# Two groups of small products on TensorE, each made one section of the schedule

## The chip, the cores and the metric

The kernel runs on one core of one Trainium2 chip. Its engines are TensorE (PE in the profile, with its weight loads as PEld), VectorE (DVE), ScalarE (ACT), GpSimd (POOL) and SyncE (SP); the last one here only issues DMAs. The metric is device time in microseconds of one execution, and the median of three runs stands for a kernel.

## What is computed

One block of a network on four sequences of 512 tokens and 256 channels: a state-space mixer with adaptive layer norm, then a gated feed-forward layer. What the change touches is the mixer's inner product. Cut to that, the reference is:

```python
Lm = jnp.exp(segsum(a))                                # decay from token s to token l, 0 for s > l
M = jnp.einsum('blhn,bshn,bhls->bhls', Cm, Bm, Lm)     # C against B over 64 states, times the decay
y = jnp.einsum('bhls,bshp->blhp', M, x)                # applied to x, 8 channels a head
```

There are 32 heads. B and C come from a projection of the normalized input, then a causal convolution over four tokens.

## The kernel before

The sum over s is cut into chunks of Q = 64 tokens. Within a chunk the product is computed as written (C times B, times the decay, times x); across chunks a state is carried. So a sequence has NC = 8 chunks.

**Tiling.** Two heads make a pair, numbered k from 0 to NP = 64: eight pairs for a unit n, which is one half of the heads of one sequence; there are eight units. Four pairs make a quad m, numbered 0 to 15. For each pair:

- `project(k, 0)` and `project(k, 1)` compute B and C: six 512-column matmuls each by `proj` (L266) into a PSUM tile (`pbc`, `pcc`), and `conv` (L400 to L407) turns each into an SBUF tile `bc` or `cc`, with two instructions on ScalarE, two on VectorE and one on GpSimd.
- `prep_l(k)` (L440) makes the decay tile `l` with one matmul and an exponential.
- `attend(k)` (L457) is called for odd k alone and takes the pairs k-1 and k. For each of 8 chunks, 2 pairs and 2 heads it issues one 64x64x64 product of C and B at one of the four 64x64 positions of the array, into the PSUM tiles `pG` of the two pairs: 32 matmuls. VectorE then multiplies each `pG` into its `l` (L473).
- `turn_b(k)` (L475) transposes `bc`, for the states.

For each quad, `intra(m)` (L552) applies the four `l` tiles to x: for each of 8 chunks and 4 pairs one matmul of 128 rows, 32 columns and 64 elements, 32 in all, into the PSUM tile `py` (L561). `states(m)` (`ps`, L545) and `inter(m)` (`pi`, L587) carry the states across chunks in the same 128x32 shape.

An FP32 matmul stands in the profile as two records, so that one `attend` or one `intra` has 64.

**Order.** The program is traced from an agenda: each step has a due time in units of one pair, from a table `T` of offsets, and is traced in order of these. The scheduler of the framework then makes each engine's queue out of this order by a simulated timeline. It may put a matmul that is ready ahead of one that was traced earlier and is not. SyncE alone keeps the order of the tracing. Where an order has to hold, the kernel adds edges by `tc.issue_after`: `behind(...)` does so for a whole step, and the class `Chain` (L268) does so from one matmul to the next within an `attend`, so that the products keep the order in which they are written; other matmuls may come between them. `intra` has no such edges.

`pl`, `pG`, `bT`, `ps`, `sT` and a few others share three PSUM buffers (`mtile`), projections share three more (`ptile`), and `py` and `pi` have one each. So the two `pG` tiles of an `attend` need two of the three shared buffers.

After the last unit the feed-forward layer follows, from about 445 us on; it has none of the steps above.

## Time and profile before

| | |
|---|---|
| median of three runs | 590.82 us (587.2 to 591.58) |
| the profiled execution | 587.27 us, its span 585.5 us |
| granted TensorE clock, mean | 0.990 |
| records of `pG` (L277) | 2048, 40.7 us busy |
| records of `py` (L561) | 1024, 29.9 us busy |
| first `pG` starts, last `py` starts | 38.8 us, 444.8 us |
| DMAs issued by SyncE | 198, on one queue; 50.58 MB |

A row of the page or of a group gives the engine, the line, the operation and its tiles (output first), the shape and the count, then busy time. Idle time of an engine stands in brackets or after the bar, with what ended it. A busy time of TensorE is not a rate, as its matmuls overlap: the 2048 records of `pG` have 222 ns each and yet only 40.7 us together. What a stage costs on TensorE is read from the starts of successive records.

### The profile page before, as it was taken

Reading aid. Unit: us, or ns where it says so; the run is one execution under the profiler, and the core shown is the slowest. Engines: PE = TensorE matmul, PEld = TensorE weight load, DVE = VectorE, ACT = ScalarE, POOL = GpSimd, SP = SyncE. Lnnn points to the kernel's source line nnn. Section 1 sums busy time; section 2 is a strip of 40 time slices with the busy share of each in tenths; the row PEclk is TensorE's granted clock in tenths of the full one; section 3 lists DMA queues with packets and bytes.
Section 4 is the critical chain, followed back from the end, with each engine's and each line's share of the span. In section 5 each row is a group of like instructions: output and inputs, shape, how many; then the busy total and the mean of one; then the engine's idle time right before and its main releaser. Section 6 shows DMA issues by size and latency. Waiting matters only on the chain.

```text
span 585.5 us, 16297 instructions
## 1 busy us (share of the span) xinstructions
PE 547.6 (94%) x6868; PEld 431.7 (74%) x6868; DVE 400.5 (68%) x668; ACT 392.8 (67%) x670; POOL 325.6 (56%) x299
## 2 busy tenths in 40 slices
PE   6887999989899999999999899899989999999996
PEld 3555776668677766877777677677767898888886
DVE  4777877877787875889787879787855454333243
ACT  6898778877967887897794887769574243232321
POOL 4773356454734578466565657477666645333341
PEclk9898999999999999999999999999989999999999
DMA  6423111210325344013203142164158046104021
GB/s 195 137 53 151 33 37 74 47 34 1 110 50 84 115 123 142 3 59 103 80 4 113 75 119 97 60 172 147 38 158 284 2 131 209 40 1 152 1 82 36
DMA packets 41792, 51.99 MB, mean 89 GB/s; under 512 B 17942, under 2 KB 29940, under 8 KB 41720
## 3 DMA queue, kind: packets, MB, share of 16 engines
q1 hardware_dynamic: 40248, 50.58, 28.6%
q8 instruction: 54, 0.88, 0.6%
q10 hardware_dynamic: 1472, 0.38, 0.3%
q14 instruction: 18, 0.15, 0.1%
HBM read 33.51 MB, written 17.44 MB: 87 GB/s over the span
## 4 chain that ended last, share of the span: by engine, by line
PE 40%; DVE 5%; ACT 4%; issue 1%; POOL 1%; DMA 1%; POOLq 0%; DVEq 0%
PE f L266 15%; PE pdy L728 4%; PE pcc L266 4%; PE pdyi L728 4%; PE pbc L266 3%; PE po L625 2%; PE pG L277 1%; PE py L561 1%; PE bT L479 1%; ACT xn L296 1%; PE ps L545 1%; PE pi L587 1%; DVE cc L405 1%; PE pt L306 1%; ACT cv L404 1%
## 5 line engine op out<-in xcount | busy, mean ns | idle before, releaser
L407 POOL TENSOR_TENSOR bc<-bc,cv 128x509 f32<-128x509 f32 x64 | 69.6, 1088 | 58.7 <-DVE bc L406 41.4
L266 PE MATMUL f<-h,wf 128*128 128x512 f32 x384 | 97.3, 395 | 0.0
L407 POOL TENSOR_TENSOR cc<-cc,cv 128x509 f32<-128x509 f32 x64 | 69.7, 1089 | 49.2 <-DVE cc L406 33.4
L266 PEld LDWEIGHTS f<-h,wf 128*128 128x128 f32 x384 | 69.0, 189 | 12.3
L721 POOL TENSOR_TENSOR fl<-ft,fh 128x512 fp32r<-128x512 f32 x31 | 40.0, 1292 | 57.6 <-ACT fh L720 52.0
L405 DVE SCALAR_TENSOR_TENSOR cc<-pcc,cw_sb,cc 128x511 f32<-128x511 f32 x64 | 47.6, 743 | 31.0 <-ACT cv L404 30.9
L402 ACT ACTIVATE cc<-pcc,cb_sb,cw_sb 128x512 f32<-128x512 f32 x64 | 50.2, 785 | 20.6 <-PE pcc L266 15.1
L266 PE MATMUL pcc<-ht,wq 128*128 128x512 f32 x192 | 55.5, 421 | 5.8 <-DVE bc L406 5.8
L402 ACT ACTIVATE bc<-pbc,cb_sb,cw_sb 128x512 f32<-128x512 f32 x64 | 50.1, 783 | 15.3 <-PE pG L277 14.0
L720 ACT ACTIVATE fh<-ft 128x512 fp32r<-128x512 f32 x32 | 20.2, 631 | 57.7 <-DVE ft L717 28.7
L716 DVE SCALAR_TENSOR_TENSOR ft<-ft,f 128x512 f32<-128x512 f32 x32 | 21.9, 687 | 52.2 <-ACT ft L715 50.0
L405 DVE SCALAR_TENSOR_TENSOR bc<-pbc,cw_sb,bc 128x511 f32<-128x511 f32 x64 | 47.6, 744 | 12.8 <-ACT cv L404 12.6
L266 PE MATMUL pcc<-hr,wq 128*128 128x512 f32 x192 | 53.3, 410 | 2.9 <-DVE bc L406 2.3
L266 PE MATMUL pbc<-ht,wq 128*128 128x512 f32 x192 | 53.0, 408 | 2.6 <-POOL wq L199 2.6
L266 PE MATMUL pbc<-hr,wq 128*128 128x512 f32 x192 | 52.4, 406 | 1.4 <-DVE cc L406 1.0
L266 PEld LDWEIGHTS pcc<-ht,wq 128*128 128x128 f32 x192 | 35.8, 196 | 18.0 <-DVE bc L406 8.0
L406 DVE SCALAR_TENSOR_TENSOR bc<-pbc,cw_sb,bc 128x510 f32<-128x510 f32 x64 | 47.6, 743 | 1.2
L406 DVE SCALAR_TENSOR_TENSOR cc<-pcc,cw_sb,cc 128x510 f32<-128x510 f32 x64 | 47.6, 744 | 1.1
L473 DVE TENSOR_TENSOR l<-pG,l 128x512 f32<-128x512 f32 x64 | 41.2, 683 | 7.8 <-PE pG L277 7.5
L479 PE MATMUL bT<-ident,bc 128*128 128x128 f32 x256 | 41.2, 283 | 4.3 <-ACT bt L481 2.6
L404 ACT ACTIVATE cv<-pbc,cw_sb 128x512 f32<-128x512 f32 x64 | 44.4, 693 | 1.4 <-POOL bc L407 0.9
L481 ACT ACTIVATE bt<-bT 128x512 f32<-128x512 f32 x64 | 38.8, 607 | 9.4 <-PE bT L479 9.2
(154 smaller groups left out, 1237.0 us busy)
## 6 DMA issues: line engine op xcount, KB each, us to landing
wq<-win_t SPq DMA_DIRECT2D x16, 256.0 KB
htd<-ht SPq DMA_DIRECT2D x8, 512.0 KB
hr<-htd SPq DMA_DIRECT2D x8, 512.0 KB
h2d<-ht SPq DMA_DIRECT2D x8, 512.0 KB
h<-h2d SPq DMA_DIRECT2D x8, 512.0 KB
x<-u SPq DMA_DIRECT2D x7, 512.0 KB
ex<-pd SPq DMA_DIRECT2D x8, 256.0 KB
ygd<-yg SPq DMA_DIRECT2D x4, 512.0 KB
```

What stands on the lines that cost most here:

```text
L266: last[pe] = pe.matmul(ps, w[:, a, k, c0 : c0 + 128], ht[k][:, b], start=(n == 0), stop=(n == 5))
L402: ac.activation(dst, ps, AF.Identity, bias=cb_sb[:, tl : tl + 1], scale=w[:, 3:4])
L404: last[ac] = ac.activation(v, ps, AF.Copy, scale=w[:, 0:1])
L405: ve.scalar_tensor_tensor(dst[:, 1:], ps[:, : S - 1], w[:, 2:3], dst[:, 1:], ALU.mult, ALU.add)
L406: last["conv"] = ve.scalar_tensor_tensor(dst[:, 2:], ps[:, : S - 2], w[:, 1:2], dst[:, 2:], ALU.mult, ALU.add)
L407: last[gp] = gp.tensor_tensor(dst[:, 3:], dst[:, 3:], v[:, : S - 3], ALU.add)
L473: ve.tensor_tensor(lts[n], pg, lts[n], ALU.mult)
L479: pe.transpose(pt[:, t], bc[:, 128 * t : 128 * t + 128], ident)
L481: ac.activation(bts[k], pt, AF.Copy)
L716: ve.scalar_tensor_tensor(t, t, 1.0, p1, ALU.add, ALU.mult)
L721: (ve if (b, f) == (NB - 1, 7) else gp).tensor_tensor(lo, t, hi.bitcast(F32), ALU.subtract)
L728: last[pe] = pe.matmul(pds[t // 2][:, t % 2], hid[a][:, tok], w2h[f][:, w_], start=(f == 0 and t % 2 == 0 and m == 0), stop=(f == 7 and m ...
```

## The change

The class `Chain` goes. In `attend` and in `intra` the loop over the products is put into `with tc.tile_critical():`, a section: the scheduler places what is in it as one unit, with nothing between. The matmuls, their operands, their order within the section, the tiles, the table `T` and all else stay as they are. There are 32 sections of `attend` and 16 of `intra`.

```diff
-    class Chain:
-        def __init__(self):
-            self.before = None
-        def matmul(self, *args, **kw):
-            with ExitStack() as order:
-                if self.before is not None:
-                    order.enter_context(tc.issue_after(self.before.ins))
-                self.before = pe.matmul(*args, **kw)
...
         pgs = [mtile([128, S], f"pG{n}") for n in ks]
-        chain = Chain()
-        for c in range(NC):
-            for n, pg in list(zip(ks, pgs))[::-1]:
-                for j in range(2):
-                    i, o = 64 * j, 64 * (j ^ (n % 2))
-                    r, l = slice(i, i + 64), slice(Q * c, Q * c + Q)
-                    chain.matmul(pg[o : o + 64, l], bcs[n][r, l], ccs[n][r, l], start=True, stop=True,
-                                 tile_position=(i, o))
+        with tc.tile_critical():
+            for c in range(NC):
+                for n, pg in list(zip(ks, pgs))[::-1]:
+                    for j in range(2):
+                        i, o = 64 * j, 64 * (j ^ (n % 2))
+                        r, l = slice(i, i + 64), slice(Q * c, Q * c + Q)
+                        pe.matmul(pg[o : o + 64, l], bcs[n][r, l], ccs[n][r, l], start=True, stop=True,
+                                  tile_position=(i, o))
...
         py = pys[n][0]
-        for c in range(NC):
-            for g in range(4):
-                l = slice(Q * c, Q * c + Q)
-                pe.matmul(py[32 * g : 32 * g + 32, l], xpad[:, pp, c, g], lts[4 * m + g][:, l],
-                          start=(pp == 0 and c == 0), stop=(pp == 1), skip_group_check=True,
-                          tile_position=(0, 32 * g))
+        with tc.tile_critical():
+            for c in range(NC):
+                for g in range(4):
+                    l = slice(Q * c, Q * c + Q)
+                    pe.matmul(py[32 * g : 32 * g + 32, l], xpad[:, pp, c, g], lts[4 * m + g][:, l],
+                              start=(pp == 0 and c == 0), stop=(pp == 1), skip_group_check=True,
+                              tile_position=(0, 32 * g))
```

## The prediction

> **What bounds the kernel now.** I read the page's first two parts, then the busy time by stretch.

> ```profile
> span 585.5 us, 16297 instructions
> PE 547.6 (94%) x6868; PEld 431.7 (74%) x6868; DVE 400.5 (68%) x668; ACT 392.8 (67%) x670; POOL 325.6 (56%) x299
> ...
> 30.00:445.00 415.00, 389.28 (x5916) 297.77 (x5914) 325.85 (x540) 328.05 (x568) 248.83 (x228) 0.99 0.29 85
> ```

> The last line is the mixer: length, then busy time of PE, PEld, DVE, ACT and POOL, the clock, the DMA share. PE is busy 389.3 of 415 us and idle 25.7; the next two engines reach 79%. PE bounds the mixer, so a microsecond given to or taken from its queue is nearly one of the span. After 445 us nothing is touched.

> How do the products stand on PE? The timeline of PE around one `attend` and around an early piece of one `intra` (start, length, line, tiles, records):

> ```profile
> 171.14 1.32 PE L266 MATMUL pz<-ht,wxz 128*128 128x512 f32 x5
> 172.39 0.33 PE L277 MATMUL pG<-cc,bc 64*64 64x64 f32 x4
> 172.65 0.74 PE L266 MATMUL pcc<-ht,wq 128*128 128x512 f32 x2
> 173.32 1.15 PE L277 MATMUL pG<-cc,bc 64*64 64x64 f32 x60
> 174.40 0.66 PE L479 MATMUL bT<-ident,bc 128*128 128x128 f32 x4
> ...
> 177.64 0.38 PE L443 MATMUL pl<-dr,dl 94*128 94x512 bf16 x1
> 177.95 0.31 PE L561 MATMUL py<-l,xpad 128*32 128x64 f32 x4
> 178.19 0.66 PE L479 MATMUL bT<-ident,bc 128*128 128x128 f32 x4
> ```

> This `attend` is cut into 4 and 60 records with projections between. Read in this way over the whole trace, 21 of the 32 attends already stand in one piece and 11 are cut like this one. `py` stands in 98 pieces. Most of its cuts are by `ps`, which has the same shape. Counting only visits to the 128x32 shape, `py` has a part in 37, for 16 intras.

> What else runs when a section would start? All engines at one `attend` that is in one piece:

> ```profile
> 103.24 1.28 POOL L611 TENSOR_TENSOR xc<-xc,zt 128x512 f32<-128x512 f32 x1
> 103.32 0.31 ACT L358 ACTIVATE spe<-spe 128x128 f32<-128x128 f32 x1
> 103.65 1.28 ACT L359 ACT_TABLE_LOAD   x1
> 103.77 1.16 PE L277 MATMUL pG<-cc,bc 64*64 64x64 f32 x64
> ```

> Neither POOL's nor ACT's instruction has to do with these products, and PE starts without them.

> [...] successive projections start 230 ns apart, but the last one before a 64x64 product 318 ns before it; after the last small product, the next matmul comes 149 ns later, against 7 to 18 within the group. [...] at the kernel's end PE's sequencer reaches its drain at 578.24 us and sits in it for 2.35 us, till the last matmul ends at 580.54; so it works some 2 us ahead of the array, and a drain takes that away. [...]

> ```profile
> L277 PEldq EVENT_SEMAPHORE x27: 51/51/51, 49.9 to 439.5; - x27
> ```

> [...] The page gives no landings, so I counted bytes: the 198 issues of SP against the packets of its queue in order of time. A DMA lands 3.3 us after its issue on average.

> **The change part by part.** No matmul is added or removed. Three things are.

> *Cuts that go.* Entering the small shape costs 318 - 230 = 88 ns and leaving it 149 - 15 = 134, with a slower start of the first records about 0.25 us a visit (`py` at 177.95: 0.24 us for four records that take 0.07 in stride, and 0.31 in place of 0.22 for the `pl` ahead). 11 attends lose one visit. Of the 37 - 16 = 21 extra visits of `py`, 15 go for sure (eight early pieces of four records, and those among `pg` and `po`); the others may stay as visits of `ps`. So 26 to 32 visits, 6.5 to 8 us: **-7 us**, all on PE.

> *Exit.* A section ends with a drain and a closing instruction on PE, and whoever waits for the products waits for the latter. No such place exists in the trace. From below it costs nothing[...]. From above it costs the latency of a matmul (218 ns), a new weight load (135) and an event (51), 0.4 us. I take 0.2: 48 x 0.2 = **+10 us** (0 to 19).

> *Entry.* This is the open step. As the scheduling library describes a section, its entry is gated by a snapshot of everything that the schedule has issued so far, on every engine and every DMA queue, and not by the inputs of the products alone. The trace has no such wait; I bound it by what is in flight at the start of the last piece of each of the 48 groups. The longest rest of a running instruction on ACT, DVE and POOL is 0.63 us on average, 30 us together: the lower bound. With the DMAs it is more: at 22 of 48 starts SP has issued bytes that are still under way (7.9 us of them at 173.32, where `ygd` and `wm` have just been issued), and the longer of the two sums to 86.5 us: the upper bound. I take the engines and half of the rest, as neighbouring sections share a late transfer and SP may run later in the schedule's order: 30 + 28 = **+58**, and 48 x 51 ns = **+2** for the last event.

> Behind PE's entry stand `bT` and the next projections. ACT's `conv` (L402) waits for those, then DVE (L405) and POOL (L407); all three run dry while PE waits, and PE catches up with none of it. But PE's own 25.7 us of idle time are waits for these engines, and mostly go if they have just caught up: **-20** (0 to -25). The scheduler also makes a new order; I know no sign for that, and put +-5 into the range.

> Sum: -7 + 10 + 58 + 2 - 20 = **+43 us**. The profiled execution took 587.27 us (span 585.5), 3.6 under the median of 590.82; I get 630 from one and 634 from the other, and say **632**. This case by itself reaches from +3 (engines only, no exit cost, all cover used) to +100 (all DMAs, the idle time kept), 594 to 690.

> **The rivals.** *The entry waits for the products' inputs alone.* For it: the data flow asks for no more, and the 21 whole attends start without a wait. Then there is -7 and +10: 591 to 594, between 583 and 604 by the bounds of the exit. *Faster, the other side:* entry and exit together cost under 7 / 48 = 0.15 us a section; from there down the saved shape changes win. The place is the end of each group, where the 149 ns to the next matmul may already be all that a drain costs. Speaking for it: PE bounds the stage and the pieces are there to be seen; against it: 2.35 us of run-ahead are given up 48 times. It gives 590.8 - 7 = 584, 579 to 589. *It does nothing much*, since 21 of 32 attends are whole already, lies inside these two.

> **How the numbers follow.** The wait for everything 0.55, for inputs alone 0.2, the faster case 0.25. One per cent (5.9 us) is about what a measurement of this kernel can tell from no change. Faster by over that: three quarters of the last case, 0.18. Within it: the rest of that, half of the second, 0.05 of the first, 0.22. Slower: 0.60. The range 582 to 680 leaves out the lower half of the faster case and the top of the first, about 0.17.

> **What would show it.** 32 pieces of 64 `pG` records and 16 of `py` confirm the grouping. If the entry waits for all, PE shows idle time ahead of `pG` and `py` that ends with engines or DMAs not among their inputs, 1 to 2 us each and longest where SP has just issued; its idle time between 30 and 445 us doubles at least, and more event instructions stand at these lines. If that idle time stays near 26 us, the entry step is wrong. If the gap after the last small product stays at 150 ns, the exit costs nothing. Should PE's busy time in the mixer fall by far more than 7 us, the count of cuts was wrong.

## The result, and the profile after

The changed kernel takes **709.78 us** (median of 5 runs, 708.58 to 711.66) against 590.82 (5 runs): a ratio of **1.202, interval 1.196 to 1.208**. The prediction of 632 had the direction, and missed the size by two thirds of the loss; 709.78 lies outside its range.

The page of the changed kernel, first its totals and the row of granted clock in 40 slices, then the answer by stretch (length; busy time of PE, PEld, DVE, ACT, POOL; clock; DMA share; GB/s):

```profile
span 709.5 us, 16967 instructions
PE 577.8 (81%) x6867; PEld 452.5 (64%) x6868; DVE 394.5 (56%) x668; ACT 395.1 (56%) x670; POOL 324.1 (46%) x299
...
PEclk8968879978998999989979999999899899999999
```

```profile
30.00:570.00 540.00, 419.29 (x5929) 319.32 (x5929) 321.86 (x543) 332.72 (x572) 249.51 (x230) 0.91 0.23 70
570.00:709.00 139.00, 134.56 (x834) 118.19 (x832) 55.34 (x90) 41.09 (x69) 59.36 (x48) 1.00 0.21 69
```

The FFN stretch is as long as before (139 against 140). All of the loss lies in the mixer, 415 to 540 us, and it has two parts. PE's idle time went from 25.7 to 120.7 us (540.00 - 419.29): **+95**. Its busy time went from 389.3 to 419.3: **+30**, for the same products. The clock explains this part: it was 0.99 in this stretch and is 0.91. Over the whole kernel the records show half clock for 104 us, before for 11. Within the mixer PE is busy for 64.9 us at half clock, before for 6.5. Work takes nearly twice as long then: successive 512-column projections start 427 ns apart at half clock and 231 at full, 128-column transposes 214 and 109. So about half of each is excess: (64.9 - 6.5) / 2 = 29 us.

Where is the idle time? PE's idle time just ahead of the first product of a `pG` or `py` piece is 92.0 us over 48 sections, and was under 0.1 us over all 141 pieces before. That is 92 of the 95. The groups of the page show the same from the other side:

```profile
L461 DVE TENSOR_TENSOR l<-pG,l 128x512 f32<-128x512 f32 x64 | 41.2, 686 | 129.5 <-PEq L452 129.5
...
L458 PEld LDWEIGHTS pG<-cc,bc 64*64 64x64 f32 x2048 | 38.5, 152 | 79.4 <-issue 79.4
```

L452 is the line that opens a section. DVE's multiplication of the finished products waits for PE's sequencer at that line, all 129.5 us of it, and the weight loads of `pG` lose 79.4 us to "issue", which is time that no semaphore of their own explains. For most of their matmuls the view of waits does name what ended last. PE's longest waits ahead of these products (line that waited, releaser, us, times, longest):

```profile
PE pG L458 <- issue: 18.2, 11, 7.9
PE pG L458 <- POOL ht L304: 8.6, 4, 2.5
PE pG L458 <- DMA de<-pend: 8.0, 1, 8.0
PE pG L458 <- DMA htd<-ht: 7.6, 1, 7.6
PE pG L458 <- DMA w2h<-w2d: 7.0, 1, 7.0
PE py L550 <- DMA dl<-p: 4.9, 1, 4.9
...
PE py L550 <- DVE parts L359: 2.1, 1, 2.1
```

The 18.2 us under "issue" hold two of the long waits, of 7.9 and 6.0 us; by the trace's semaphore updates they end when the transfers `dl` and `pend` land. `pG` is a product of `cc` and `bc`. It reads none of `ht`, `de`, `htd`, `dl` or `w2h`; the last are weights of the FFN. So the wait is for other work that was under way. The timeline around the wait for `de` shows how far this goes (start, length, engine, line; in brackets the idle time before it):

```profile
153.79 0.61 ACT L434 ACTIVATE l<-pl 128x512 f32<-128x512 f32 x1
156.18 0.36 SPq L477 DMA_DIRECT2D de<-pend  x1
160.51 1.24 PE L458 MATMUL pG<-cc,bc 64*64 64x64 f32 x36 [8.01 <-DMA de<-pend]
```

PE has waited since 152.5. ACT, the last engine at work, stops at 154.40. The transfer that ends the wait is issued only at 156.18, 3.7 us after the wait began: SP itself had to wait until `pend` had been written. For six microseconds (154.4 to 160.5) no compute engine works at all.

What does the wait consist of? The program puts six event instructions ahead of each section, and then a branch. Each event waits on two semaphores, out of eight that count SP's transfers and four that engines raise; the branch waits for POOL. The trace has the start of each (554 event instructions on PE, 132 before) and the updates of each semaphore. A wait ends 28 to 35 ns after an update of one of the two, so it can be put down to that one:

| PE's idle time ahead of 48 sections, us | sum | each |
|---|---|---|
| waiting for transfers | 41.3 | 0.86 |
| waiting for ACT 8.2, DVE 5.7, POOL 4.4 | 18.3 | 0.38 |
| stepping from one event to the next, 0.106 each | 18.0 | 0.37 |
| from the branch to the first product | 11.3 | 0.23 |
| not assigned | 3.1 | |
| sum | 92.0 | 1.9 |

The third and fourth rows are paid even where all other work is done: PE's queue still waits for PE's own last matmul and then steps through what remains. In 20 of the 48 entries this is all or nearly all, 0.43 to 0.60 us. The seven longest entries, of 4.2 to 8.0 us and mostly for transfers, make up 46 of the 92 us. The second row is not divided between inputs of the products and other work.

Not everything in flight is waited for. The section at 566.96 us starts after 0.44 us of idle time while four transfers, issued from 559.33 on, land only at 567.23 to 569.79. The same holds at one more section of the 48. Scheduling is done ahead of the run, on a simulated timeline; it seems that a section waits for what stands ahead of it there.

The branch is a `COMPARE_BRANCH` in the trace. Its 48 records last 163 to 290 ns each, and it is 234 ns on average from the start of the record to the first product. The first weight load is no part of that, since its record starts with the product's.

At the exit the line of the section shows the drain that the prediction expected (instruction, count, shortest/median/longest ns):

```profile
L452 PEldq DRAIN  x32: 277/328/715, 51.1 to 562.8; - x32
L546 PEldq DRAIN  x16: 307/499/1088, 79.9 to 567.8; - x16
```

PE idles for 6.2 us in all just after the last product of a `pG` piece, before for 0.3.

### The profile page after: what moved, and what is told of

Its sections match the earlier page's. It is cut to its first block, busy times and chain, and to the rows that moved or that the text cites. A ratio compares the mean times of both kernels' runs of the same rounds, so it can differ in the third digit from the quotient of the medians.

```text
span 709.5 us, 16967 instructions
## 1 busy us (share of the span) xinstructions
PE 577.8 (81%) x6867; PEld 452.5 (64%) x6868; DVE 394.5 (56%) x668; ACT 395.1 (56%) x670; POOL 324.1 (46%) x299
## 5 line engine op out<-in xcount | busy, mean ns | idle before, releaser
L461 DVE TENSOR_TENSOR l<-pG,l 128x512 f32<-128x512 f32 x64 | 41.2, 686 | 129.5 <-PEq L452 129.5
L458 PE MATMUL pG<-cc,bc 64*64 64x64 f32 x2048 | 43.3, 241 | 67.7 <-issue 18.2
L266 PE MATMUL f<-h,wf 128*128 128x512 f32 x384 | 95.9, 394 | 0.0
L458 PEld LDWEIGHTS pG<-cc,bc 64*64 64x64 f32 x2048 | 38.5, 152 | 79.4 <-issue 79.4
L266 PEld LDWEIGHTS f<-h,wf 128*128 128x128 f32 x384 | 69.3, 189 | 12.9 <-DVE bc L395 0.2
L266 PE MATMUL pcc<-ht,wq 128*128 128x512 f32 x192 | 56.2, 430 | 2.4 <-DVE bc L395 1.7
L266 PE MATMUL pbc<-ht,wq 128*128 128x512 f32 x192 | 53.4, 413 | 4.5 <-POOL wq L199 1.9
L266 PE MATMUL pcc<-hr,wq 128*128 128x512 f32 x192 | 54.4, 420 | 1.1 <-DVE bc L395 1.1
L266 PE MATMUL pbc<-hr,wq 128*128 128x512 f32 x192 | 53.5, 415 | 1.4 <-DVE cc L395 0.8
L467 PE MATMUL bT<-ident,bc 128*128 128x128 f32 x256 | 48.2, 305 | 7.1 <-PEq L452 3.0
L567 POOL TENSOR_TENSOR sts<-sn,own 128x448 f32<-128x448 f32 x16 | 16.1, 1006 | 73.1 <-DVE sn L563 72.4
```

The lines of the kernel that those rows point to most:

```text
L266: last[pe] = pe.matmul(ps, w[:, a, k, c0 : c0 + 128], ht[k][:, b], start=(n == 0), stop=(n == 5))
L458: pe.matmul(pg[o : o + 64, l], bcs[n][r, l], ccs[n][r, l], start=True, stop=True, tile_position=(i, o))
L461: ve.tensor_tensor(lts[n], pg, lts[n], ALU.mult)
L467: pe.transpose(pt[:, t], bc[:, 128 * t : 128 * t + 128], ident)
```

## The experiments

The theory after the result: **a section's entry waits for work under way on all engines and queues, costs some steps of its own, and with the idle time the clock falls to half (104 us of it above).** Rivals: the gathering of the products or the new order is what costs; only the transfers matter; only the engines matter.

**Sections without the gathering.** The kernel before, chains and order of pairs as they were, with a section of a single one-column product ahead of each group (for the C-B products it writes a column that they overwrite):

```
+        with tc.tile_critical():
+            pe.matmul(pgs[1][:, :1], idle[:, :128], idle[:, :1], start=True, stop=True)
         chain = Chain()
...
+        ps = mtile([128, 1], f"dm{m}")
+        with tc.tile_critical():
+            pe.matmul(ps, idle[:, :128], idle[:, :1], start=True, stop=True)
```

> The kernel before, products ordered as before, but with a section of one single-column product (on zeros, into a tile that is overwritten or never read) ahead of each of the 48 groups. The entry waits for everything issued so far: the waits come back without any grouping, 48 entries of about 2 us and a slower clock, 680 to 720 us, with 80 to 120 us of new idle time on PE ahead of the one-column products. Rival, the grouping or the new order of the matmuls costs the time: 48 x 0.3 us for drains and little else, 595 to 610 us.

Measured: 688.62 us, ratio 1.167 (1.157 to 1.176). Waits of PE in its profile:

```profile
PE dm L562 <- DMA de<-pend: 6.9, 1, 6.9
PE dm L562 <- DMA ex<-pd: 5.8, 1, 5.8
...
PE dm L562 <- DMA h2d<-ht: 5.0, 1, 5.0
```

`dm` multiplies a constant by itself, and yet waits 5 to 7 us for transfers that have nothing to do with it. (The view names the transfer of the latest update. By the semaphores on which the events waited, the first two waits ended with `ex` and `wq`.) A section by itself, with nothing gathered, brings 98 us, against 119 in the changed kernel. The time is as expected, its make-up is not: PE idles for 66 us ahead of the one-column products where 80 to 120 were expected. In the mixer (30 to 550 us) PE's idle time grows by 63 us and its busy time by 42, and the half clock accounts for 25 of these 42. The other 17 come with the added products and were not taken apart. So this run shows the wait and its effect on the clock without any gathering. How much of the changed kernel's loss the gathering may still hold can't be read from it.

**The gathering without sections.** Here the products of a group stand in one piece by edges of issue order alone, and all PE work that comes later in the kernel's text stays behind it (`Fenced` issues every PE instruction after the one in `fence[0]`):

```
+    pe = Fenced()
...
+    def in_turn(*args, **kw):
+        fence[0] = pe.matmul(*args, **kw)
...
-                    chain.matmul(pg[o : o + 64, l], bcs[n][r, l], ccs[n][r, l], ...)
+                    in_turn(pg[o : o + 64, l], bcs[n][r, l], ccs[n][r, l], ...)
```

> The kernel before with the grouping made by issue-order edges alone: each product of a group follows the one before, and every PE instruction traced later follows the last of the group; no section, no entry. If the entry's wait is the cost: 583 to 597 us. Rival, the grouping or its order is the cost: 640 us or more, as the attends then stand in 33 pieces in place of 43 with nothing gained.

Measured: 620.32 us, ratio 1.050 (1.045 to 1.056), between the two. The waits are now of another kind:

```profile
PE py L92 <- DVE xpad L540: 15.9, 10, 5.3
PE pG L92 <- POOL cc L416: 10.3, 7, 2.7
```

Both are inputs of the products. Because PE may not go ahead with later work, it stands still until `xpad` or `cc` is there. That is the fence's doing and has no part in the changed kernel, where later work may be placed ahead of a section. So this run does not price the gathering cleanly; a milder form follows below.

**Each half alone.** The change in `attend` only, and in `intra` only:

> The change in attend alone (32 sections), intra as before. In the changed kernel's trace the entries of attends hold 73 us and those of intras 28 us, so the entry theory gives about 3/4 of the loss here: 660 to 700 us. The rival (grouping) gives little, since 21 of 32 attends were whole already: under 610 us.

> The change in intra alone (16 sections), attend as before. Entry theory: about a quarter of the loss, 612 to 640 us. Rival (grouping): most of the loss, since intra had been cut into the most pieces: 660 us or more.

Measured: 679.63 (1.151, 1.143 to 1.160) and 645.42 (1.093, 1.086 to 1.101), the second a little over its range. The 32 sections cost 89 us, the 16 cost 54, each 2.8 and 3.4. Together that is 143, more than the 119 of both. The likely reason is that neighbouring sections share a late transfer: in both profiles the view names `de<-pend` for PE's longest waits, 16.2 us in the first and 14.1 in the second (by the semaphores, `ex` or `de` of the same fetch), and the changed kernel has 8.0 us under that name.

**What a section costs by itself.** The changed kernel, with every section of C-B products opened twice:

```
-        with tc.tile_critical():
-            for c in range(NC):
+        for cs in (range(0, NC // 2), range(NC // 2, NC)):
+            with tc.tile_critical():
+              for c in cs:
```

> The changed kernel, with every section of C-B products opened twice, for chunks 0 to 3 and for chunks 4 to 7: 32 more sections and no more work. Theory (a section has a fixed cost of its own): in the changed kernel's profile the shortest entries, with everything long done, still cost 0.6 us, and the exit 0.33; the second half finds little in flight, so 32 x 0.95 = 30 us more, with a few us of half clock on top: 735 to 755 us. Rival (all of an entry is waiting for work in flight, which the first half has already waited out): 32 second entries for nothing, 708 to 716 us.

Measured: 770.79 us, 1.309 (1.300 to 1.317) times the kernel before; 61 us more than the changed kernel where 30 and a few were expected. Its mixer:

```profile
30.00:631.00 601.00, 453.64 (x5930) 337.94 (x5931) 325.38 (x544) 334.13 (x572) 250.01 (x231) 0.87 0.21 63
```

Idle time over the whole span went from 131.7 to 157.8 us, +26, and busy time from 577.8 to 612.4, +35. Of the latter the half clock is +28 (half of 127.1 us busy at half clock, less 35.9). Without the clock an extra section costs (61 - 28) / 32 = 1.0 us, as expected; with the clock it is 61 / 32 = 1.9. The 32 second entries hold 28.5 us of idle time, 6.9 of it for transfers, and the shortest takes 0.43 us again. At 28 of them the scheduler has put other matmuls between the two halves, mostly transposes. The theory's steps hold and its few us of half clock were far too low.

**Transfers moved away.** The changed kernel with two groups of transfers later in the order of work, and the kernel before with the same move:

```
-        x_proj=1.32, x0=-1.5, ...
+        x_proj=1.32, x0=-0.7, ...
-        load_w2=63.01, ...
+        load_w2=65.5, ...
-        at_time(8 * n + T["x0"] if n else 1.2, x_fetch, n)
+        at_time(8 * n + T["x0"] if n else 1.9, x_fetch, n)
```

> The changed kernel, with two groups of transfers moved in the order of work so that no section follows them closely: the fetch of the next batch element's input (0.7 to 0.8 of a schedule unit later) and the load of the second FFN weight (after the last section). Theory (an entry waits for every transfer queued before it in the order of work, which is half of the entry time): the waits that end with those loads are some 7 us for the weight and 10 to 20 for the inputs, so 685 to 702 us. Rival (transfers only happen to end last, and the engines' queues and fixed steps would take their place): 704 to 714 us.

> The kernel before, with the same two groups of transfers moved as in the run with late transfers. Theory: without a section nobody waits for these transfers as a group, so the move is worth nothing here: 586 to 596 us. Rival (the move helps or hurts by itself, since data come later or queues get shorter): outside 583 to 600 us, and the run with late transfers has to be read against that.

Measured: 703.69 (1.191, 1.184 to 1.198) and 593.03 (1.0035, 1.0008 to 1.0062). The move gains 6 us with sections, about 1%, where the intervals of the two ratios just touch; without sections it loses 3 against the kernel before of the same measurement (590.23), as its theory allowed. With sections the time falls between what the theory and the rival said. The waits named after `w2h` (7.0) and `x` (4.2) are gone, but PE's idle time for transfers only falls from 41.3 to 39.5 us. Other late transfers take most of the place: the wait for `ex` and `de` is 9.9 us where it was 8.0, and one of 2.8 us for `de` and `w2a` is new.

**Transfers added.** A transfer of 64 KB ahead of each of the 32 C-B groups, in both kernels; nobody reads the copy:

```
         pgs = [mtile([128, S], f"pG{n}") for n in ks]
+        copy = dram.tile([128, 128], F32, name=f"copy{k}")
+        nc.sync.dma_start(copy, ccs[k][:, :128])
```

> The changed kernel, with one more transfer of 64 KB ahead of each of the 32 sections of C-B products in the order of work: a part of the last input of the products is copied to DRAM, where nobody reads it. Theory (a section waits for every transfer queued ahead of it): the last input is ready 0.7 us before the products as a rule, and a transfer takes 2 us and more to land, so 0.5 to 2 us more at most of the 32 entries, and a few us of half clock: 725 to 765 us. Rival (transfers merely happen to end last; nobody waits for one that feeds nothing): 704 to 716 us.

> The kernel before, with the same 32 transfers, so that their own cost is known. Both theories: no instruction waits for them but the next writer of the input's buffer, which is long after, so 588 to 598 us. If it lies above 605, the transfers cost something without a section as well, and the run with sections has to be read against that.

Measured: 707.25 (1.198, 1.194 to 1.202) and 599.17 (1.015, 1.011 to 1.019). Both miss what the theory said: with sections the time is that of the changed kernel, inside the rival's range, and without them the transfers cost 9 us. But the trace doesn't bear out the rival's reason. The view of waits names a copy twice:

```profile
PE pG L460 <- DMA copy<-cc: 6.5, 1, 6.5
...
PE py L552 <- DMA copy<-cc: 2.8, 1, 2.8
```

Neither wait is a copy's. At the first, the event that PE's queue stood at passes at 226.75 us, 29 ns after the last update by `pend`, and the product starts at 227.61, while the copy lands at 229.17; at the second the updates are those of `w2h`. It is at ten other sections that an event passes within 60 ns of a copy's landing, after PE's queue has waited 0.6 to 1.3 us for it. So a section does wait for a copy that nobody reads. It costs little because a copy mostly lands 1.5 us after its issue, where 2 us and more were expected (in the changed kernel 184 of SP's 198 transfers take that long to land), and PE has matmuls left to run meanwhile: of the 10.0 us for which the queue waits, PE idles for 1.2. And six of the 32 sections start before their copy has landed, four of them before it is even issued; so it is again the scheduler's order that counts, and not all that is in flight.

PE's idle time for transfers is 34.0 us here, against 41.3. So the number of transfers doesn't matter here. The seven or so that are late do, some because SP waits for data first (as for `de`), some probably because they queue behind large ones: `dl`, 48 KB, was issued at 355.68 in the changed kernel, behind transfers of up to 512 KB, and landed at 363.43.

**A milder gathering, no section.** The kernel before, with its chain also in `intra` and the pairs in an order that leaves no early piece:

```
+        chain = Chain()
         for c in range(NC):
-            for g in range(4):
+            for g in (3, 2, 1, 0):
...
-                pe.matmul(py[32 * g : 32 * g + 32, l], xpad[:, pp, c, g], lts[4 * m + g][:, l],
+                chain.matmul(py[32 * g : 32 * g + 32, l], xpad[:, pp, c, g], lts[4 * m + g][:, l],
```

> The kernel before, with the chain of issue order that it has for the C-B products also on the products within chunks, in an order of pairs that leaves no early piece; no section. Theory (the gathering itself is a small gain, the section is the loss): visits to the 128x32 shape fall from 35 to 26, 9 x 0.25 = 2 us less, 586 to 590 us with the kernel before at 590. Rival (gathering the products holds PE up for the last pair's input, as some us of the loss of the run that was grouped without sections): 595 to 605 us.

Measured: 589.76 us, ratio 1.0006 (0.998 to 1.003). The gain of 2 us is not to be seen, nor a loss. In the profile, visits with `py` fell from 37 to 27, ten of the 21 that could go; 10 of the 32 attends are still cut. Half clock covers 23 us in it, against 11, but the kernel before itself has granted clocks from 0.976 to 0.997 from run to run, so one profile can't tell whether the gathering did that. No version here beats the kernel before.

Giving the changed kernel's exact order to a kernel without sections was not tried. So the share of the new order is bounded from outside only: the entries hold 92 of the 95 us of added idle time, and of the waits in them at most the 18 us for engines can be waits for inputs that came late by the order.

## Why the prediction was right and wrong

Right: a wait for other work that is under way, at 48 places, on the engine that bounds the stage; PE's idle time more than doubled; `pG` stands in 32 pieces of 64 and `py` in 16 visits; waits that end with engines and transfers that are no inputs. The rivals (entry for inputs alone, 591 to 594; faster, 584; nothing) fall with the first experiment. The sum, term by term, against the mixer's +125:

| step of the prediction | predicted | measured |
|---|---|---|
| cuts that go, with the exit | -7 + 10 = +3 | 1 + 6 = +7 |
| entry, work in flight | +58 | 41.3 + 18.3 = +60 |
| "for the last event" | +2 | 18.0 + 11.3 = **+29** |
| not assigned in the entry | - | +3 |
| PE's own idle time absorbed | -20 | **-3** |
| clock | not in the sum | **+29** |
| sum | +43 | +125 |

*Cuts and exit.* At full clock the median gap from the last small product to the next matmul went from 149 to 330 ns, by 0.18 us where 0.2 was taken. That an exit may cost nothing, the lower bound, was the author's estimate. PE's idle time there grew by 6 us (0.3 to 6.2). What is left of the busy time after the clock is +1, so a gain of 7 us from cuts that go is not to be seen.

*In flight.* The sum was met, the parts were not: transfers 41 instead of 28, engines 18 instead of 30. That the sum fits is luck. Counting what was in flight at the start of the old pieces missed a transfer like `de` that stood queued on SP, not yet issued. It also took a landing at 3.3 us after the issue, from bytes; by the last update of its semaphore a transfer of SP lands 4.7 us after its issue on average in the trace before. Waits for engines were shorter, and at 20 entries little but PE's own last matmul was waited for. (The lower end of the range, +3, isn't its own terms either: -7 + 30 + 2 - 25 is 0.)

*The step that failed first* is "48 x 51 ns" for the event. It priced one instruction by its record. A section here has six events one after the other, 0.106 us apart, of which 3.5 on average fall into PE's idle time, and then a branch that takes 0.23 us to the first product: 0.61 us, twelve times as much.

*The second* is that idle time would be absorbed. Leaving out the entries and what follows `pG`, PE's waits in the mixer were 25.4 us and are 22.5. The engines that PE waited for stand behind the same sections; ACT's longest waits ahead of `bc`, before and after:

```profile
ACT bc L402 <- PE pG L277: 14.0, 14, 1.8
ACT bc L391 <- PEq L452: 82.4, 29, 10.3
```

So these engines don't get ahead while PE waits, and after an entry PE has to wait for them as before.

*The third* is a term that was never put down. The view by stretch gave the clock as 0.99, and the prediction treated it as a constant. With 29 us it is nearly a quarter of the loss.

## What to carry to other kernels

A section that the scheduler keeps whole is a barrier against what the schedule has placed ahead of it on every engine and queue, not a hint about order: price it as events, branch and drain (here about 1.0 us even with little in flight), plus the wait for the latest transfer, each time (here 0.86 us on average, and up to 8.0). Where only order is wanted, use edges of issue order, and first count how many pieces are split at all; here joining a part of them was worth nothing measurable. The name that a view gives to the end of a wait is inferred; where an argument rests on it, compare it with the updates of the semaphores. And when a change puts gaps into the engine that bounds a stage, add its clock to the sum (here 29 of 125 us).
